# One ring of eight slots for the softmax weights of three attentions, with a planner that counts the slots

## The chip, the core and the metric

The kernel runs on one core of a Trainium2 chip. The metric is the device time of one execution in microseconds (us), as the median of several runs. Everything is computed in 32-bit floats.

## The reference

The input x is 8 images of 64 x 64 pixels with 256 channels. Two layers follow each other.

```
# layer 0
qkv = x @ w_qkv + b_qkv            # 256 -> 512, q and k; v is k
ctx_h = sdpa over 8 horizontal windows of 8 rows, channels 0..127, 4 heads of 32
ctx_v = sdpa over 8 vertical windows of 8 columns, channels 128..255, 4 heads of 32
hv  = hard_swish(v)
context = hard_swish(concat(ctx_h, ctx_v) + depthwise_conv3x3(hv) + dw_bias)
x = context @ w_out + b_out
# layer 1
f, g, h = x @ kf + bf, x @ kg + bg, x @ kh + bh     # 256 -> 32 each, spectrally normed
beta = softmax(g @ f.T)            # 4096 x 4096 per image
out = gamma * ((beta @ h) @ kv + bv) + x
```

Each window has 512 pixels, so a window of a head is a 512 x 512 attention. Layer 1 is a 4096 x 4096 attention with 32 channels.

## The kernel before

Scores are made transposed: keys stand on the 128 partitions, queries on the columns. A **step** is one block of 128 keys against 512 queries for four heads (layer 0) or four blocks of queries (layer 1), so 2048 columns of scores. In each step TensorE makes the scores in PSUM, ScalarE (ACT) turns them into weights with exponentials of 1024 columns each, TensorE multiplies the weights with the values into one accumulator `num`, and the sum of the weights is gathered for the division at the end. For an image there are

- 8 **h units** (horizontal windows, scores at L787, values at L816), 4 steps each, names `p_h`, `acc_h`, `num_h`, `sum_h`;
- 8 **v units** (vertical windows, scores at L764 and L787, values at L809 and L816). They have 3 steps: step 0 is as above with 2048 columns, steps 1 and 2 (`passes`) have 3072, written in three passes of 256 queries. Such a step uses three pairs of PSUM banks, `first`, `mid` and `last`, and gives two tiles of weights: `p_v` with 2048 columns (L776, L777) and the middle one `p_v_m` with 1024 (L781);
- 2 **l units** (layer 1, scores at L994, values at L1010), 32 steps each.

PSUM has six banks as three pairs for scores, one bank for the accumulator `num` and one, `mm`, for every other product. The scores of a step can only be written once the exponential has emptied their pair.

**Weights in SBUF before.** The pool `ptp` holds three buffers of 2048 columns (tag `pt`) for all steps in turn, and one of 1024 (tag `pm`) for the middle tile. A buffer may be written again when every reader of its last tile is done. Readers are: the value product (L809, L816, L1010); DVE's adds into `acc` (L825 `add` in h and v, L832 `add_mid` in v, L1025 in l), of which there is only one buffer as well; TensorE's sums with a matrix of ones (L847), which in v read step 2 and its middle tile directly; and in l the gather of the fourth row block by a DMA from POOL's queue that adds in flight into `acc_l` or `row_l` (L1036).

**Other work around it.** The projections of the next images (L298, tile `pq`), the depthwise convolution (nine taps, the first on ACT at L692, eight on DVE at L696), the hard swish, the normalizations (L558 to L561, L864), the joined context (L888 to L897), the projections to f, g and h (L917, L944) and the output (L298 into the score banks, then L1076) are put between the steps. f, g and h are staged in tiles with the tag `fgh` (two buffers of 512 columns; L926, L952) and copied on by DMA or transposed; output tiles have the tag `ot` (two buffers of 512 columns; L1076, L1103) and are stored by DMA.

**Order.** Image by image the units run h1 to h7, v0 to v7, then h0 of the next image, then l0 and l1. The program is written under a manual schedule, so each engine runs its instructions in the order in which the Python code issues them. A planner, the class `Flow`, sets that order: it keeps a modelled clock for each engine with fixed costs (in us: `SCORES`, `VALUES`, `EXP`, `ADD` and so on; `GATHER` and `SUMMED` for the gather by DMA), holds tasks with due times in lanes, and after each step fills the time until the PSUM banks come free. `step` issues scores and exponentials of a step, then the values of the step before, then the rest. For the middle tile, the exponential is issued by `rest` after those values.

Before it issues a step, the planner must have issued every reader of the tile that the new one takes the place of. It calls `flow.require` for the readers of step `t - 3`, and for the middle tile for those of the last middle tile. These readers are then in the order, but the modelled clock of ACT does not wait for their end: the exponential is modelled to end `EXP` after the scores or after ACT's last work.

Of the kernel before, what the change touches and what calls it, by code (L numbers as in the profile page):

```python
# [11 lines left out]
F32 = mybir.dt.float32  # L12
# [5 lines left out]
P = 128  # L18
# [3 lines left out]
TB = 512  # L22
NB = N // TB
D = 32
# [16 lines left out]
def side(h):  # L41
# [3 lines left out]
QH = 4  # L45

DUE = dict(
    near_k=-4, near_q=0, near_values=-14, clip=-12, swish=-1,
# [13 lines left out]
ADD, ADD3, NORM, SWISH, TAP, TAPS = 2.36, 1.83, 2.5, 0.75, 0.75, 1.28  # L62
GATHER, SUMMED = 1.0, 3.0
PE_LAG, LAG, SLACK = 0.28, 0.1, 0.3
# [3 lines left out]
class Task:  # L68
# [4 lines left out]
    def __init__(self, pieces, due=0, needs=(), after=(), ready=0, bank=False):  # L73
        self.pieces, self.due, self.ready = deque(pieces), due, ready
        self.needs, self.after, self.bank = list(needs), list(after), bank
        self.done, self.end = False, 0.0
        self.then = None
        self.ends = False

    def begin(self):  # L80
# [6 lines left out]
class Flow:  # L87
# [5 lines left out]
    def __init__(self):  # L93
        self.t = 0
        self.clock = dict(pe=0.0, act=0.0, dve=0.0, sp=0.0)
        self.lanes = dict(pe=[], turn=[], act=[], dve=[], sp=[], pool=[], rows=[], res=[])
        self.open = None
        self.held, self.held_more, self.values_due = None, 0.0, False
        self.bank_free = 0.0
        self.half_end = self.exp_end = 0.0  # L100
        self.third = False
        self.apart = 0
# [7 lines left out]
    def run(self, task):  # L110
        now = self.begin(task)
        fn, chain = task.pieces.popleft()
        fn()
        if task.then and len(task.pieces) <= task.then[0]:
            task.due = task.then[1]
        if task.lane == "sp":
            now = max(now, self.clock["pe"])
        for engine, took in chain:
            if engine in self.clock:
                now = max(now, self.clock[engine])  # L120
                self.clock[engine] = now + took
            now += took + (PE_LAG if engine == "pe" else LAG)
            if task.bank and engine in ("act", "dve"):
                self.bank_free = now
        task.end = now
        if task.bank:
            self.open = task if task.pieces else None
        if not task.pieces:
            task.done = True
            self.lanes[task.lane].remove(task)  # L130
# [5 lines left out]
    def require(self, *tasks):  # L136
        for task in tasks:
            task, left = task if isinstance(task, tuple) else (task, 0)
            while not task.done and len(task.pieces) > left:
                self.require(*task.needs, *task.after)  # L140
                if task.bank and self.open not in (None, task):
                    self.require(self.open)
                self.run(task)

    def waiting(self, lane):
# [79 lines left out]
    def step(self, scores, values, passes=2, third=False):  # L225
# [17 lines left out]
        if scores:  # L243
            rest = scores()
            c["pe"] = max(c["pe"], self.banks()) + DRAIN + SCORES + more
            self.third = third
            self.half_end = max(c["act"], c["pe"] - more + PE_LAG) + EXP
            if more:
                self.half_end = max(self.half_end, c["pe"] + PE_LAG) + EXP
            before, self.exp_end = self.exp_end, self.half_end + EXP  # L250
            c["act"] = self.exp_end
        else:
            before = self.exp_end
            c["pe"] = self.half_end = self.exp_end = max(c["pe"], c["act"], c["dve"]) + 3.0
# [11 lines left out]
        if rest:  # L266
            rest()
        self.fill_act(self.late(c["pe"]) - EVICT)
        self.fill_pe()
# [32 lines left out]
def tile_attention_blocks(  # L302
# [163 lines left out]
    def attention(images, load_x, out_rows, exact):  # L466
# [19 lines left out]
        f4 = state.tile([P, N], F32, name="f4")  # L486
        gq = state.tile([P, 2, TB], F32, name="gq")


# [54 lines left out]

        def weights_of(sc, name, scale):
            pt = ptp.tile([P, NQ, TB], F32, tag="pt", name=name)
            for z in range(2):
                nc.scalar.activation(pt[:, 2 * z : 2 * z + 2, :], sc[z], AF.Exp, scale=scale)  # L548
            return pt
# [40 lines left out]
        def image(b):  # L590
# [136 lines left out]
            def window_unit(kind, i):  # L727
# [26 lines left out]
                def scores(c):  # L754
                    q, k = sources(kind, i)
                    if exact and c == 0:
                        maxima()
                    name = f"p_{nm}_{c}"
                    if c in passes:
                        first, mid, last = sc = [pairs.popleft() for _ in range(3)]  # L760
                        pairs.extend((first, last, mid))
                        for n, (t, h) in enumerate(passes[c]):
                            for r in range(NQ):
# [9 lines left out]
                                if n == 2 and r == 0:  # L773
                                    handed(mm, relay)
                        pt = ptp.tile([P, NQ, TB], F32, tag="pt", name=name)
                        nc.scalar.activation(pt[:, :2, :], first, AF.Exp, scale=D**-0.5)  # L776
                        nc.scalar.activation(pt[:, 2:, :], last, AF.Exp, scale=D**-0.5)  # L777

                        def rest():
                            pm = ptp.tile([P, 2, TB], F32, tag="pm", name=f"{name}_m", bufs=1)  # L780
                            nc.scalar.activation(pm, mid, AF.Exp, scale=D**-0.5)  # L781
                            u[c], u["mid", c] = pt, pm
# [3 lines left out]
                    for r in range(NQ):  # L786
# [5 lines left out]
                        if exact:  # L792
# [4 lines left out]
                            )  # L797
                    u[c] = weights_of(sc, name, D**-0.5)
                    return None
# [107 lines left out]
            def fgh_tile(name):  # L907
                return work.tile([P, TB], F32, tag="fgh", name=f"{name}_{b}")

# [55 lines left out]
            def global_unit(z):  # L965
# [23 lines left out]
                def scores(c):  # L989
# [3 lines left out]
                    for r in range(NQ):  # L993
# [4 lines left out]
                        if exact:  # L998
# [4 lines left out]
                            )  # L1003
                    u[c] = weights_of(sc, f"p_{nm}_{c}", 1.0)

# [150 lines left out]

        readers = defaultdict(list)
        last_users = dict(acc=[], sum=[])
# [5 lines left out]
        def weights_ready(t):  # L1164
            task = Task([])
            task.done, task.step = True, t
            weights[t] = task
            return task

        weights = {}  # L1170
        for u in units:
# [32 lines left out]
            else:  # L1204
# [238 lines left out]

        mids = []
# [22 lines left out]
        with tc.manual_schedule():  # L1467
# [3 lines left out]
            for n, (u, c) in enumerate(steps):  # L1471
# [6 lines left out]
                if u.kind:  # L1478
                    weights[u.t + c].end = flow.exp_end + LAG
            if not exact:  # L1480
# [83 lines left out]
```

## Time and profile before

| | us |
|---|---|
| median of 3 runs | 3411.5 |
| lowest and highest | 3410.2, 3414.52 |
| the profiled execution | 3416.69 |
| its span on the core | 3414.9 |
| TensorE (PE) busy | 3309.1 (97%) |
| DVE busy | 2662.5 (78%) |
| ACT busy | 2669.1 (78%) |
| POOL busy | 518.4 (15%) |

The profile is of one execution, which was 5.2 us slower than the median of the runs shown; its span leaves out 1.8 us around it. Matmuls overlap and their ends are modelled, so a busy PE isn't PE at its peak: where that matters, the distance between starts is read. The granted TensorE clock had a mean of 0.994. "Idle before" a group of instructions is the time in which its engine stood still just before them, put down to what ended the wait.

### The profile page before, as it was taken

The numbers are of one execution on the slowest core, as the hardware profiler recorded it, in microseconds if no ns is written. First come the engines' busy times: TensorE is split into PE (matmuls) and PEld (weight loads), VectorE is DVE, ScalarE is ACT, GpSimd is POOL, SyncE is SP. The second block draws the span as 40 slices with busy tenths as digits, with TensorE's granted clock in tenths as the row PEclk, the third lists the DMA queues.
The fourth block names the chain that finished last, engine by engine and source line by source line (L and its number), as shares of the span: only waits on it lengthen the run. The fifth ranks groups of instructions, "written<-read, shape, count | busy, mean of one in ns | idle before, by whom it ended". The sixth has DMA issues, their size and how long they took to land. (4 is left out here: it accounts for less than half of the span.)

```text
span 3414.9 us, 82562 instructions
## 1 busy us (share of the span) xinstructions
PE 3309.1 (97%) x35348; PEld 1197.4 (35%) x35348; DVE 2662.5 (78%) x2404; ACT 2669.1 (78%) x3235; POOL 518.4 (15%) x776
## 2 busy tenths in 40 slices
PE   7889999999999999999999999999999999999998
PEld 3343333443334333343333433334333343333422
DVE  5778679876898758887598966988769886699865
ACT  5677787787877878778788787878877888778776
POOL 0001230012300123002230022200222003210032
PEclk9999999999999999999999999999999999999999
DMA  2123653245622555225552255423654236542365
GB/s 71 51 81 96 124 122 90 69 115 122 121 84 75 117 125 113 88 74 117 130 110 81 87 123 117 110 70 96 122 124 107 62 98 134 117 99 63 99 122 110
DMA packets 321111, 344.35 MB, mean 101 GB/s; under 512 B 34272, under 2 KB 198624, under 8 KB 320736
## 3 DMA queue, kind: packets, MB, share of 16 engines
q0 software_dynamic: 71680, 134.25, 22.3%
q1 hardware_dynamic: 246816, 204.18, 20.2%
q8 instruction: 280, 4.59, 0.6%
q10 hardware_dynamic: 2240, 0.56, 0.1%
q14 instruction: 95, 0.78, 0.1%
HBM read 99.78 MB, written 83.89 MB: 54 GB/s over the span
## 5 line engine op out<-in xcount | busy, mean ns | idle before, releaser
L548 ACT ACTIVATE p_l<-s 128x1024 f32<-128x1024 f32 x1024 | 994.0, 1027 | 175.4 <-PE s L994 137.6
L1025 DVE TENSOR_TENSOR acc_l<-acc_l,p_l 128x1536 f32<-128x1536 f32 x480 | 843.6, 1758 | 362.6 <-ACT p_l L548 357.8
L696 DVE SCALAR_TENSOR_TENSOR act<-hv,dw_sb,act 128x1024 f32<-128x1024 f32 x512 | 654.8, 1279 | 10.1
L994 PE MATMUL s<-gq,f 32*128 32x512 f32 x4096 | 616.2, 640 | 3.6 <-ACT p_l L548 3.4
L548 ACT ACTIVATE p_h<-s 128x1024 f32<-128x1024 f32 x512 | 495.6, 1023 | 104.3 <-PE s L787 70.4
L1010 PE MATMUL num_l<-p_l,h_sb 128*32 128x512 f32 x4096 | 546.3, 605 | 1.9 <-ACT nums_l L1040 1.9
L298 PE MATMUL pq<-x,wqkv_sb 128*32 128x256 f32 x8192 | 533.4, 381 | 12.8 <-ACT kv L641 8.4
L298 PEld LDWEIGHTS pq<-x,wqkv_sb 128*32 128x32 f32 x8192 | 264.3, 110 | 398.8 <-issue 250.2
L787 PE MATMUL s<-qh,kh 32*128 32x512 f32 x2048 | 307.1, 641 | 6.5 <-ACT qh L622 5.7
L1036 POOL DMA_DIRECT2D row_l<-p_l x240 | 219.1, 913 | 549.8 <-ACT p_l L548 493.0
L994 PEld LDWEIGHTS s<-gq,f 32*128 32x128 f32 x4096 | 179.7, 183 | 289.1 <-issue 270.6
L1036 POOL DMA_DIRECT2D acc_l<-p_l x240 | 211.0, 879 | 441.7 <-ACT p_l L548 406.3
L816 PE MATMUL num_h<-p_h,vs 128*32 128x512 f32 x2048 | 273.6, 606 | 3.8 <-DMA vs<-kvia 3.0
L764 PE MATMUL s<-qv,kv 32*128 32x256 f32 x3072 | 228.9, 399 | 4.1 <-ACT p_v L548 2.6
L298 PE MATMUL s<-act,wout_sb 128*32 128x512 f32 x2048 | 227.6, 594 | 0.2 <-ACT ot_l L1103 0.2
L1010 PEld LDWEIGHTS num_l<-p_l,h_sb 128*32 128x32 f32 x4096 | 80.7, 108 | 387.2 <-issue 372.6
L825 DVE TENSOR_TENSOR acc_h<-p_h,p_h 128x2048 f32<-128x2048 f32 x64 | 146.5, 2289 | 89.5 <-ACT p_h L548 51.7
L781 ACT ACTIVATE p_v_m<-s 128x1024 f32<-128x1024 f32 x128 | 131.6, 1028 | 98.8 <-DVE acc_v L832 59.5
L809 PE MATMUL num_v<-p_v,vs 128*32 128x256 f32 x2048 | 203.7, 390 | 0.0
L1076 ACT ACTIVATE ot_l<-s,bias_o 128x512 f32<-128x512 f32 x120 | 76.0, 685 | 151.0 <-PE s L298 143.1
L825 DVE TENSOR_TENSOR acc_v<-p_v,p_v 128x2048 f32<-128x2048 f32 x64 | 146.6, 2291 | 52.2 <-PE sum_v L847 45.0
L764 PEld LDWEIGHTS s<-qv,kv 32*128 32x128 f32 x3072 | 147.9, 185 | 95.2 <-issue 50.3
(146 smaller groups left out, 3551.8 us busy)
## 6 DMA issues: line engine op xcount, KB each, us to landing
acc_l<-p_l POOLq DMA_DIRECT2D x256, 256.0 KB, 3.4
row_l<-p_l POOLq DMA_DIRECT2D x256, 256.0 KB, 3.3
x<-in_xT SPq DMA_DIRECT2D x92, 512.0 KB, 4.1
kvia<-kt SPq DMA_DIRECT2D x128, 256.0 KB, 2.5
vs<-kvia SPq DMA_DIRECT2D x512, 64.0 KB, 2.1
out<-ot_l SPq DMA_DIRECT2D x128, 256.0 KB, 2.1
via_v<-nums_v SPq DMA_DIRECT2D x64, 256.0 KB, 2.1
shuf_v<-via_v SPq DMA_DIRECT2D x256, 64.0 KB, 2.1
```

The source lines that it names most:

```text
L298: nc.tensor.matmul(out[quad(r), :], lhsT=lhsT[:, quad(r)], rhs=rhs, start=start, stop=stop)
L548: nc.scalar.activation(pt[:, 2 * z : 2 * z + 2, :], sc[z], AF.Exp, scale=scale)
L696: nc.vector.scalar_tensor_tensor(o, src, wt, o, ALU.mult, ALU.add)
L764: mm = nc.tensor.matmul(place_of(n, r, h, sc), lhsT=k[quad(r), t * P : (t + 1) * P], rhs=q[quad(r), side(h)], start=True, stop=True,)
L787: nc.tensor.matmul(row_of(sc, r), lhsT=k[quad(r), c * P : (c + 1) * P], rhs=q[quad(r), :], start=True, stop=not exact,)
L809: nc.tensor.matmul(u["num"][quad(r), side(h)], lhsT=vs[kind, i][:, r, t, :], rhs=place_of(n, r, h, (pt[:, :2], u["mid", c], pt[:, 2:])), s ...
L816: nc.tensor.matmul(u["num"][quad(r), :], lhsT=vs[kind, i][:, r, c, :], rhs=u[c][:, r, :], start=(c == 0), stop=(c == 3),)
L825: nc.vector.tensor_add(u["acc"], u["acc"] if c == 2 else u[0], u[c])
L994: nc.tensor.matmul(row_of(sc, r), lhsT=f4[quad(r), c * P : (c + 1) * P], rhs=gq[quad(r), z, :], start=True, stop=not exact,)
L1010: nc.tensor.matmul(u["num"][quad(r), :], lhsT=h_sb[:, c, :], rhs=u[c][:, r, :], start=(c == 0), stop=(c == 4 * NB - 1),)
L1025: nc.vector.tensor_add(acc, u[0][:, :rows, :] if c == 1 else acc, u[c][:, :rows, :])
L1036: nc.gpsimd.dma_start(out=u["row", c % 2], in_=u[c][:, rows, :], accum_op=ALU.add)
```

## The change

All weights lie in one tile `weights` of eight slots of 1024 columns. A step takes two slots that follow each other; a step with passes takes three, and in a v unit these are laid out so that step 0 has slots 0 and 1, step 1 slots 2 and 3 with its middle in 4, step 2 slots 6 and 7 with its middle in 5. Eight slots of 4 KB take 32 KB of a partition. The three buffers of 8 KB and the one of 4 KB took 28; the 4 KB of the two `fgh` buffers are the rest, and f, g and h are now staged in the two `ot` buffers.

The planner walks the steps once ahead of time, gives each its slots, and notes for each slot which earlier step last had it and whether as a middle tile. Before a step it requires the readers of exactly those; `require` now also returns when they end by the modelled clock, and the end of the exponentials is modelled to be no earlier (`weights_free` for the first two, `mid_free` for the middle one). As a task can have several pieces, the end of each piece is noted in `times`. The costs `GATHER` and `SUMMED` of the model are set from 1.0 and 3.0 to 0.9 and 2.6.

```diff
+SLOTS = 8
-GATHER, SUMMED = 1.0, 3.0
+GATHER, SUMMED = 0.9, 2.6
...
-        task.end = now
+        task.end = task.times[len(task.pieces)] = now
...
     def require(self, *tasks):
...
+        ends = [k[0].times.get(k[1], k[0].end) if isinstance(k, tuple) else k.end for k in tasks]
+        return max(ends, default=0.0)
...
-            self.half_end = max(c["act"], c["pe"] - more + PE_LAG) + EXP
+            self.half_end = max(c["act"], c["pe"] - more + PE_LAG, self.weights_free) + EXP
...
         if rest:
             rest()
+            if self.mid_free > self.exp_end - EXP:
+                self.exp_end = c["act"] = self.mid_free + EXP
...
-        ptp = pools.enter_context(tc.tile_pool(name=f"ptp{sfx}", bufs=3))
...
+        weights = state.tile([P, SLOTS, 2, TB], F32, name="p")
...
+        def weights_at(slot, n=2):
+            return weights[:, slot : slot + n].rearrange("p s i c -> p (s i) c")
+
-            pt = ptp.tile([P, NQ, TB], F32, tag="pt", name=name)
+            pt = weights_at(next(slots)[0])
...
-                            pm = ptp.tile([P, 2, TB], F32, tag="pm", name=f"{name}_m", bufs=1)
+                            pm = weights_at(mid_at, 1)
...
-                return work.tile([P, TB], F32, tag="fgh", name=f"{name}_{b}")
+                return work.tile([P, TB], F32, tag="ot", name=f"{name}_{b}", bufs=out_bufs)
...
-                for c, task in enumerate((pair, pair, *held)):
+                first = (pair, 1) if u.passes else pair
+                for c, task in enumerate((first, first, *held)):
                     readers[u.t + c].append(task)
                 if u.passes:
-                    u.mids = {1: pair, 2: (total, 2) if acc is pair else acc}
+                    last_mids[u.t + 1] = pair
+                    last_mids[u.t + 2] = (total, 2) if acc is pair else acc
...
+        taken, order, old, place_at = {}, [], [], 0
+        for u in units:
+            for c in range(u.steps if u.kind else 0):
+                n = u.t + c
+                if u.kind in ("h", "v") and c in u.passes:
+                    at, mid_at = (place_at, place_at + 2) if c == 1 else (place_at + 1, place_at)
+                    place_at += 3
+                else:
+                    at, mid_at = place_at, None
+                    place_at += 2
+                assert place_at <= SLOTS
+                place_at %= SLOTS
+                order.append((at, mid_at))
+                before = [], []
+                for k, (slot, kept) in enumerate(((at, (n, 0)), (at + 1, (n, 0)), (mid_at, (n, 1)))):
+                    if slot is not None:
+                        if slot in taken:
+                            before[k // 2].append(taken[slot])
+                        taken[slot] = kept
+                old.append((n, before))
...
-                flow.require(*u.ahead.get(c, ()), *readers.pop(u.t + c - 3, ()))
+                flow.require(*u.ahead.get(c, ()))
+                flow.weights_free = flow.require(*left_by(old[u.t + c][0]))
...
-                flow.require(*mids)
-                mids[:] = [u.mids[c]]
+                flow.mid_free = flow.require(*left_by(old[u.t + c][1]))
                 rest()
```

More of the change, by code (lines that the diff above doesn't have):

```diff
@@ L78, in __init__ @@
         self.ends = False
+        self.times = {}
     def begin(self):
@@ L100, in __init__ @@
         self.half_end = self.exp_end = 0.0
+        self.weights_free = self.mid_free = 0.0
         self.third = False
@@ L487, in attention @@
         gq = state.tile([P, 2, TB], F32, name="gq")
+        weights = state.tile([P, SLOTS, 2, TB], F32, name="p")
+        slots = iter(())
         pairs = deque(ps_sc.tile([P, 2, TB], F32, name=f"s_{i}") for i in range(3))
@@ L543, in row_of, with weights_of @@
             return sc[r // 2][:, r % 2, :]
-        def weights_of(sc, name, scale):
-            pt = ptp.tile([P, NQ, TB], F32, tag="pt", name=name)
+        def weights_at(slot, n=2):
+            return weights[:, slot : slot + n].rearrange("p s i c -> p (s i) c")
+        def weights_of(sc, scale):
+            pt = weights_at(next(slots)[0])
             for z in range(2):
@@ L757, in scores @@
                         maxima()
-                    name = f"p_{nm}_{c}"
                     if c in passes:
@@ L774, in scores @@
                                     handed(mm, relay)
-                        pt = ptp.tile([P, NQ, TB], F32, tag="pt", name=name)
+                        at, mid_at = next(slots)
+                        pt = weights_at(at)
                         nc.scalar.activation(pt[:, :2, :], first, AF.Exp, scale=D**-0.5)
@@ L797, in scores @@
                             )
-                    u[c] = weights_of(sc, name, D**-0.5)
+                    u[c] = weights_of(sc, D**-0.5)
                     return None
@@ L1003, in scores @@
                             )
-                    u[c] = weights_of(sc, f"p_{nm}_{c}", 1.0)
+                    u[c] = weights_of(sc, 1.0)
                 def weighted(c):
@@ L1154, in attention @@
                 place(u, "l")
-        readers = defaultdict(list)
+        readers, last_mids = defaultdict(list), {}
         last_users = dict(acc=[], sum=[])
@@ L1166, in weights_ready @@
             task.done, task.step = True, t
-            weights[t] = task
+            made[t] = task
             return task
-        weights = {}
+        made = {}
         for u in units:
@@ L1442, in attention, with left_by @@
                     load(nxt, i, *near, nxt.far[i, 1], nxt.far[i, 3])
-        mids = []
+        taken, order, old, place_at = {}, [], [], 0
[18 more added lines that the diff above has]
+                old.append((n, before))
+        old = dict(old)
+        slots = iter(order)
+        def left_by(kept):
+            return [k for n, mid in kept for k in ([last_mids[n]] if mid else readers[n])]
         def unit_scores(u, c):
             if u.kind:
-                flow.require(*u.ahead.get(c, ()), *readers.pop(u.t + c - 3, ()))
+                flow.require(*u.ahead.get(c, ()))
+                flow.weights_free = flow.require(*left_by(old[u.t + c][0]))
                 if exact and c == 0 and flow.open:
@@ L1478, in attention @@
                 if u.kind:
-                    weights[u.t + c].end = flow.exp_end + LAG
+                    made[u.t + c].end = flow.exp_end + LAG
             if not exact:
```

## The prediction

> **What bounds the kernel now.** I began with the page's first part, the busy shares of the engines:
>
> ```profile
> PE 3309.1 (97%) x35348; PEld 1197.4 (35%) x35348; DVE 2662.5 (78%) x2404; ACT 2669.1 (78%) x3235; POOL 518.4 (15%) x776
> ```
>
> TensorE looks full, but this is a mean over stages that repeat eight times, and matmul ends are modelled. So I cut out one image, the fourth, at the first exponential of each stage, and asked for the busy time in three stretches: h (horizontal windows, 28 steps), v (vertical, 24 steps) and l (global attention, 64 steps).
>
> ```profile
> 1358.90:1466.80 107.90, 105.89 (x1068) 35.44 (x1060) 97.51 (x96) 83.12 (x101) 0.68 (x5) 1.00 0.25 77
> 1466.80:1563.30 96.50, 93.58 (x1232) 44.94 (x1232) 81.34 (x90) 76.62 (x92) 0.33 (x3) 0.98 0.30 86
> ...
> 1576.70:1775.40 198.70, 197.53 (x1992) 63.52 (x1992) 141.78 (x101) 161.89 (x198) 62.03 (x85) 1.00 0.61 124
> ```
>
> The columns are length, then PE, weight load, DVE, ACT and POOL busy. PE is near the whole length everywhere, so this alone separates nothing. What separates the stages is the distance from start to start on PE. In l it is tight:
>
> ```profile
> 1601.99 1.07 PE L1010 MATMUL num_l<-p_l,h_sb 128*32 128x512 f32 x8
> 1602.88 0.61 PE L298 MATMUL pq<-x,wqkv_sb 128*32 128x256 f32 x8
> 1603.42 1.14 PE L994 MATMUL s<-gq,f 32*128 32x512 f32 x8
> 1604.49 1.06 PE L1010 MATMUL num_l<-p_l,h_sb 128*32 128x512 f32 x8
> ```
>
> Values take 0.89 us, a projection piece 0.54, scores 1.07, and nothing lies between. Priced this way, l's 1992 matmul records are 1024 of scores and values (1.96 us per 16, 125 us), some 144 of the output product (an estimate from the page's counts, 2048 and 240 over eight images, half in l; 0.11 each, 16 us) and some 824 short ones (0.54 to 0.97 us per 8 to 16, so about 0.063 each, 52 us): 193 of 198.7 us. TensorE bounds l, with at most 6 us to win.
>
> In v it is not tight. One unit of the steady stretch, the starts on PE:
>
> ```profile
> 1510.01 1.58 PE L764 MATMUL s<-qv,kv 32*128 32x256 f32 x24
> ...
> 1512.95 1.36 PE L787 MATMUL s<-qv,kv 32*128 32x512 f32 x8
> 1514.24 0.63 PE L809 MATMUL num_v<-p_v,vs 128*32 128x256 f32 x4
> 1515.01 0.64 PE L809 MATMUL num_v<-p_v_m,vs 128*32 128x256 f32 x8
> ...
> 1516.42 2.15 PE L764 MATMUL s<-qv,kv 32*128 32x256 f32 x24
> 1518.51 1.07 PE L816 MATMUL num_v<-p_v,vs 128*32 128x512 f32 x8
> ...
> 1521.66 1.58 PE L764 MATMUL s<-qv,kv 32*128 32x256 f32 x24
> ```
>
> The period is 11.65 us. The same 24 score matmuls take 1.50 us at 1510.01 (values begin at 1511.51) and 2.09 at 1516.42. The 24 value matmuls take 1.44 us at 1511.51 and 2.18 at 1514.24, with a hole before 1515.01, where they need the middle weights p_v_m. So 0.59 + 0.74 + about 0.2 (the 512-column scores, 1.29 against 1.07) = 1.5 us of the period is waiting, and 10.1 is work. ScalarE at that place:
>
> ```profile
> 1513.93 1.02 ACT L781 ACTIVATE p_v_m<-s 128x1024 f32<-128x1024 f32 x1 [0.80 <-DVE acc_v L832]
> ```
>
> The exponential of the middle pair has its scores, but its buffer is the only one of its kind and DVE's add has not left it. ACT starts it 0.80 us late, the two exponentials behind it slip as well, and PE waits for all three. ACT's waits over the whole run (us in total, times, longest):
>
> ```profile
> ACT p_v_m L781 <- DVE acc_v L832: 59.5, 61, 3.0
> ACT p_v_m L781 <- PE sum_v L847: 37.9, 40, 1.3
> ...
> ACT p_h L548 <- DVE acc_h L825: 31.3, 26, 1.9
> ...
> ACT p_l L548 <- DMA acc_l<-p_l: 15.0, 9, 2.0
> ...
> ACT p_l L548 <- DVE acc_l L1025: 8.9, 11, 1.2
> ...
> ACT p_l L548 <- DMA row_l<-p_l: 4.7, 7, 1.6
> ```
>
> These six are the waits for a weight buffer, 157 us; every other large wait of ACT is for PE's results and has nothing to do with the change.
>
> **The change part by part.**
>
> *Ring instead of three big buffers and one small.* Eight slots of 1024 columns: a v unit uses 2 + 3 + 3 = 8, an h unit 4 x 2 = 8, an l step 2. A middle slot is reused three steps later where it was one or two, an h or l slot four steps later where it was three. No activation, matmul or add is added or removed.
>
> v, the wait behind acc_v (59.5 us): the middle slot of step 2 was last read a unit (about 11 us) ago, so the wait goes. Following the unit above by hand: the middle exponential starts at 1513.13 and not 1513.93, its values no longer hold PE (0.74 back), and the next exponentials come 0.8 earlier, which gives most of the 0.59 back, because PE then waits for the last bank only. What is late next is ACT's last exponential and DVE. I take 0.75 to 0.8 of a us per unit, 64 units: 48 to 51 us.
>
> v, the wait behind sum_v (37.9 us): it goes too, but at 1519.39 to 1521.66 PE is busy with the sums without a gap, and the exponential released is needed only after them. The cover is those sums; I take 0. If the cover were gone it could bring 38.
>
> h (31.3 us): ACT stands there 26 times, DVE being the late one, busy 97.5 of 107.9 us. Half reaches PE, as PE is nearly full: 12 us taken, between 0 and 31.
>
> l (15.0 + 8.9 + 4.7 = 28.6 us): PE is never short in the rows above. Taken: 4 us, between 0 and 28.6. Here a rule weighs against my reading. The Trainium skill, page "Perfetto Trace Analysis", section "Identifying the Most-Contended Engine", says not to judge TensorE's headroom by matmul busy time but by the weight-load share. That share is 63.5/198.7 = 32% in l and 44.9/96.5 = 47% in v, so by the rule l has more room than v and its 28.6 us could come back in full. The start-to-start row says at most 6 us per image for everything. I follow the row; by the rule the sum would be some 25 us larger.
>
> *Waits on ACT's queue.* With one tile, every exponential and not only the first of a tile has its own list of earlier readers and writers. In the built programs ACT has 2204 semaphore instructions after and 1245 before, and 759 exponentials (138 before) have TensorE's signal in such an instruction ahead of them and a wait for an older activation, eight or more back and long done, in themselves. Nothing new is waited for. What an instruction of this kind costs:
>
> ```profile
> L548 ACTq EVENT_SEMAPHORE  x688: 17/38/2767, 36.6 to 3381.2; - x172
> ```
>
> 17 or 38 ns where nothing is outstanding, and it runs under the activation before it. Where ACT really waits for PE, the trace shows an activation 22 ns after PE's signal if it waits itself, and 45 ns after the end of the semaphore instruction if that one waits: some 0.04 us more. Exponentials released by PE are 478 in ACT's waits (263 + 127 + 88); with 759/2048 of all in the slow form, 177 x 0.045 = 8 us. Ends: 0 (all hidden) and 759 x 0.045 = 34 us. I take +8.
>
> *f/g/h staging in the result buffers.* Two result buffers of the same size serve both. Results (L1076) are written in the second half of l and the first half of h; in the image above they stop before 1410 and begin again after 1674, and f/g/h (L926, L952) lie between 1527 and 1599. The gap of over 70 us on either side hides the handover; 51 more semaphore instructions are in the count above. 0 us; if the two met, one store's landing (2.1 us) per tile.
>
> *Planner.* GATHER and SUMMED fall to 0.9 and 2.6: the trace has 0.87 us per gather and 3.3 to landing. In the built program the order on PE within v is as before. Per image, 16 matmul instructions (one projection, 4 x 0.43 = 1.7 us) move from h to l; on DVE five taps leave h, four go to v and one to l, and one normalization (0.71 + 0.25 + 0.71 + 0.69 = 2.36 us) moves from v to h. DVE in h: 97.5 - 6.4 - 0.7 (a swish) + 2.4 = 93; in v: 81.3 + 5.1 - 2.4 = 84. On PE the move is even, h loses what l gains. In v DVE also puts the normalization of the unit before ahead of the add, which makes it wait for ACT's copy of the sums, about 0.7 us per unit: 84 + 6 = 90 us per v stage. That is the next bound: 96.5 - 6 = 90.5, what the wait removed gives. SP's and POOL's queues keep their DMAs, 1506 and 512.
>
> Sum: -49 (v) - 12 (h) - 4 (l) + 8 (semaphores) = -57. The profiled execution took 3416.7 us (span 3414.9), 5.2 above the median 3411.5; 3416.7 - 57 - 5.2 = 3354.5, so 3355 us.
>
> **The rivals.**
>
> *DVE takes over in v.* For it: 84 us of work plus waits in a stage that shall last 90. If half of v's and h's gain is lost so: -25 - 6 + 8 = -23, 3389 us. Against it: acc_v is needed only at the next unit's sums, some 3 us later even in the new order.
>
> *More than the sum.* If h's and l's waits reach the end in full and v gets its 1.5 us per unit: v 96 and h and l 8 more than forecast, with semaphores hidden: about -105, 3307 us. Against it: no stage of h or l shows such holes on PE.
>
> *Slower: the semaphore instructions.* Place: ACT ahead of each exponential that waits for PE, in l and h above all, where PE waits for the bank that ACT empties. Price: up to 34 us; the projection moved into l, which is full, adds 1.7 x 7 = 12. It decides once v returns less than 46 us, that is under 0.7 us per unit with h and l giving nothing; with 0.45 per unit (29 us) the run is 17 us longer, 3428. Against it: those instructions mostly run ahead, under an activation of 1.02 us.
>
> *No change:* the new wait is for DVE at the same places. Only if both effects cancel, 3411.
>
> **How the numbers follow.** Forecast 0.66 (3330 to 3382), DVE in v 0.13, more 0.09, slower 0.08, no change 0.04. Differences under 0.2% (7 us) can't be told from none. The range 3315 to 3398 holds the forecast and the DVE case and part of the larger gain; left out are slower, no change and the far end. Faster is 0.66 + 0.13 + 0.09 = 0.88, same 0.04, slower 0.08.
>
> **What would show it.** Right: ACT's waits for acc_v and sum_v at the middle exponential are nearly gone, v lasts 90 to 91 us, a steady unit about 10.8, l within 2 us of 198.7, h 104 to 107. DVE in v above 90% of the stage. Wrong: v unchanged with ACT or PE waiting for DVE there; or l longer by 4 us or more per image with activations late behind semaphore instructions; or h shorter by far more than 4 us.

## Result and profile after: faster, by a third of the forecast

The changed kernel takes 3392.97 us (median of 5 runs, 3392.09 to 3395.03) and the one before 3411.5 (5 runs): ratio 0.9947, 95% interval 0.9933 to 0.9962. That is 18.5 us less where 57 were forecast. The profiled span is 3390.2 us.

The busy shares of the page of the changed kernel say nothing about the place:

```profile
PE 3295.3 (97%) x35348; PEld 1196.2 (35%) x35348; DVE 2658.9 (78%) x2404; ACT 2662.6 (79%) x3235; POOL 557.5 (16%) x776
```

The fourth image again, in four stages: h, v, the four steps of the next image's h unit (called h0), and l. The stretches that the prediction shows lie 11 us too late. In the kernel before, the first exponential of v is this one, and not one at 1466.8:

```profile
1455.78 1.94 ACT L548 ACTIVATE p_v<-s 128x1024 f32<-128x1024 f32 x2
```

All borders are off by the same 11 us, so the lengths hold, but the busy times are those of other stretches. Cut at the first exponentials, the kernel before has

```profile
1347.90:1455.80 107.90, 106.04 (x1044) 33.76 (x1042) 93.87 (x90) 83.59 (x104) 4.31 (x11) 1.00 0.28 83
1455.80:1552.30 96.50, 92.89 (x1220) 45.21 (x1216) 86.25 (x94) 75.74 (x92) 0.33 (x3) 0.98 0.30 85
1552.30:1565.70 13.40, 13.35 (x148) 5.12 (x148) 8.22 (x10) 11.11 (x15) 0.00 (x0) 1.00 0.26 73
1565.70:1764.40 198.70, 198.13 (x2008) 63.88 (x2006) 143.06 (x106) 162.60 (x199) 60.46 (x82) 1.00 0.61 126
```

and the changed one (the columns are length, PE, weight load, DVE, ACT, POOL)

```profile
1340.20:1442.50 102.30, 102.07 (x1012) 32.40 (x1010) 88.08 (x86) 80.53 (x100) 4.91 (x7) 1.00 0.28 83
1442.50:1535.80 93.30, 91.03 (x1192) 44.90 (x1192) 88.01 (x93) 76.09 (x93) 0.33 (x3) 1.00 0.29 86
1535.80:1552.70 16.90, 15.76 (x184) 5.94 (x180) 8.18 (x9) 11.91 (x16) 0.00 (x0) 1.00 0.20 51
1552.70:1753.50 200.80, 200.39 (x2038) 64.96 (x2030) 146.78 (x113) 163.51 (x200) 66.36 (x86) 1.00 0.62 128
```

v looks 3.2 us shorter, but it has 28 matmul records fewer (1192 against 1220), and h0 has 36 more and is 3.5 us longer: that is work that crossed the border. The two must be read together, 109.9 before and 110.2 after. They gained nothing. h is 5.6 us shorter, 1.7 of it the projection that went to l, and l 2.1 us longer.

The six waits for weight buffers of before have become these (ACT's waits: us in total, times, longest):

```profile
ACT sum_sb_v L580 <- PE sum_v L859: 45.8, 40, 2.1
ACT p L560 <- DVE acc_v L837: 35.5, 29, 3.4
...
ACT p L560 <- DVE acc_l L1037: 21.2, 13, 2.5
ACT p L560 <- DVE acc_h L837: 19.3, 16, 3.1
```

The waits at the middle exponential (97 us before) are gone but for 0.4 us, as forecast. In their place the exponentials of step 0 (L560) wait for the add into acc_v, 35.5 us, and the copy of the sums waits 45.8 us (9.4 before).

The fourth v unit, v3, shows how. First TensorE, from its step-0 values to the next unit's:

```profile
1480.45 1.06 PE L828 MATMUL num_v<-p,vs 128*32 128x512 f32 x8
...
1489.32 0.70 PE L775 MATMUL s<-qv,kv 32*128 32x256 f32 x4
1490.28 0.71 PE L775 MATMUL s<-qv,kv 32*128 32x256 f32 x8 [0.26 <-ACT p L560]
1491.20 1.13 PE L775 MATMUL s<-qv,kv 32*128 32x256 f32 x12 [0.20 <-ACT p L560]
1492.26 1.07 PE L828 MATMUL num_v<-p,vs 128*32 128x512 f32 x8
```

The period is 11.81 us; the same unit took 11.69 before. The 24 score matmuls come in three bits, each after an exponential, and take 2.94 us where 1.5 is enough. Then ACT in the same stretch:

```profile
1483.79 0.59 ACT L580 COPY sum_sb_v<-sum_v 128x512 f32<-128x512 f32 x1 [1.22 <-PE sum_v L859]
...
1489.20 1.94 ACT L560 ACTIVATE p<-s 128x1024 f32<-128x1024 f32 x2 [0.90 <-DVE acc_v L837]
```

and DVE, whose order explains both:

```profile
1484.41 0.71 DVE L570 STREAM_TRANSPOSE zt_v<-sum_sb_v 128x512 f32<-128x512 f32 x1 [0.24 <-ACT sum_sb_v L580]
1485.16 0.26 DVE L572 RECIPROCAL recs<-zt_v 128x16 f32<-128x16 f32 x1
1485.45 0.71 DVE L573 STREAM_TRANSPOSE sum_sb_v<-recs 128x512 f32<-128x512 f32 x1
1486.19 0.69 DVE L876 TENSOR_TENSOR nums_v<-nums_v,sum_sb_v 128x512 f32<-128x512 f32 x1
1486.80 2.29 DVE L837 TENSOR_TENSOR acc_v<-p 128x2048 f32<-128x2048 f32 x1
```

The normalization of the unit before now stands ahead of the add that reads step 0's and step 1's weights; the exponential of the next step 0 needs the slots that this add leaves. So there is a closed loop: sums on PE end (1483.7), copy on ACT (to 1484.4), normalization (to 1486.8), add (to 1489.1), two exponentials (to 1491.1), last scores (to 1492.3), values and sums (to 1495.5). From one end of the sums to the next, 11.8 us. No engine needs to be full for it. DVE is nearly full in this unit all the same (the third busy time, 11.36 of 11.81 us):

```profile
1480.45:1492.26 11.81, 11.35 (x146) 5.49 (x144) 11.36 (x13) 9.23 (x12) 0.00 (x0) 1.00 0.31 94
```

So a full DVE looks as likely a cause as the loop; the light taps below decide between the two. Three of the eight v units, v1 to v3, have this period.

### The profile page after: what moved, and what is told of

It is laid out like the page before. It is cut to its first block, busy times and chain, and to the rows that moved or that the text cites. A ratio compares the mean times of both kernels' runs of the same rounds, so it can differ in the third digit from the quotient of the medians.

```text
span 3390.2 us, 83413 instructions
## 1 busy us (share of the span) xinstructions
PE 3295.3 (97%) x35348; PEld 1196.2 (35%) x35348; DVE 2658.9 (78%) x2404; ACT 2662.6 (79%) x3235; POOL 557.5 (16%) x776
## 4 chain that ended last, share of the span: by engine, by line
PE 80%; DVE 9%; ACT 5%; issue 3%; DMA 1%; SPq 0%; ACTq 0%; DVEq 0%
PE s L1006 15%; PE num_l L1022 13%; PE pq L306 12%; PE s L799 9%; PE s L306 7%; PE num_h L828 6%; PE s L775 4%; PE sum_v L859 4%; PE sum_h L859 3%; DVE act L708 3%; ACT p L560 3%; PE num_v L821 3%; DVE acc_v L837 2%; PE num_v L828 2%; PE pf L929 1%
## 5 line engine op out<-in xcount | busy, mean ns | idle before, releaser
L560 ACT ACTIVATE p<-s 128x1024 f32<-128x1024 f32 x1664 | 1611.7, 1025 | 295.5 <-PE s L1006 144.5
L1037 DVE TENSOR_TENSOR acc_l<-acc_l,p 128x1536 f32<-128x1536 f32 x480 | 842.9, 1756 | 346.9 <-ACT p L560 342.8
L1022 PE MATMUL num_l<-p,h_sb 128*32 128x512 f32 x4096 | 546.5, 605 | 1.9 <-ACT nums_l L1052 1.9
L1048 POOL DMA_DIRECT2D row_l<-p x240 | 211.1, 879 | 505.1 <-ACT p L560 483.9
L1048 POOL DMA_DIRECT2D acc_l<-p x240 | 212.6, 886 | 447.7 <-ACT p L560 388.8
L828 PE MATMUL num_h<-p,vs 128*32 128x512 f32 x2048 | 273.3, 605 | 4.6 <-DMA vs<-kvia 2.7
L775 PE MATMUL s<-qv,kv 32*128 32x256 f32 x3072 | 251.4, 402 | 18.5 <-ACT p L560 16.8
L837 DVE TENSOR_TENSOR acc_h<-p 128x2048 f32<-128x2048 f32 x64 | 146.2, 2284 | 111.6 <-ACT p L560 62.3
L821 PE MATMUL num_v<-p,vs 128*32 128x256 f32 x3072 | 192.3, 383 | 0.0
L837 DVE TENSOR_TENSOR acc_v<-p 128x2048 f32<-128x2048 f32 x64 | 146.4, 2287 | 28.1 <-ACT act L704 15.4
L837 DVE TENSOR_TENSOR acc_h<-acc_h,p 128x2048 f32<-128x2048 f32 x64 | 146.0, 2282 | 13.1 <-ACT p L560 13.1
```

The costliest lines, as they stand in the source:

```text
L775: mm = nc.tensor.matmul(place_of(n, r, h, sc), lhsT=k[quad(r), t * P : (t + 1) * P], rhs=q[quad(r), side(h)], start=True, stop=True,)
L821: nc.tensor.matmul(u["num"][quad(r), side(h)], lhsT=vs[kind, i][:, r, t, :], rhs=place_of(n, r, h, (pt[:, :2], u["mid", c], pt[:, 2:])), s ...
L828: nc.tensor.matmul(u["num"][quad(r), :], lhsT=vs[kind, i][:, r, c, :], rhs=u[c][:, r, :], start=(c == 0), stop=(c == 3),)
L837: nc.vector.tensor_add(u["acc"], u["acc"] if c == 2 else u[0], u[c])
L1022: nc.tensor.matmul(u["num"][quad(r), :], lhsT=h_sb[:, c, :], rhs=u[c][:, r, :], start=(c == 0), stop=(c == 4 * NB - 1),)
L1037: nc.vector.tensor_add(acc, u[0][:, :rows, :] if c == 1 else acc, u[c][:, :rows, :])
```

## The experiments

All times per image below are means over the second to seventh image, read from each kernel's trace between the first exponentials of the stages.

| kernel | us | h | v + h0 | l | image | first image |
|---|---|---|---|---|---|---|
| before | 3411.5 | 108.0 | 109.7 | 199.0 | 416.7 | 514.5 |
| after | 3393.0 | 102.3 | 110.2 | 200.8 | 413.4 | 513.5 |
| ring, old order | 3351.2 | 105.9 | 105.1 | 198.1 | 409.1 | 500.3 |
| old buffers, new planner | 3435.9 | 103.3 | 112.6 | 204.8 | 420.7 | 513.3 |
| two middle buffers, old order | 3360.6 | 108.0 | 103.1 | 199.1 | 410.2 | 506.3 |
| after, acc_v first | 3356.5 | 102.4 | 105.4 | 200.9 | 408.7 | 510.3 |
| after, mid requirement back | 3354.4 | 102.4 | 102.9 | 201.5 | 406.8 | 518.4 |
| after, no slot clock | 3374.0 | 104.9 | 105.4 | 198.9 | 409.2 | 521.7 |
| after, norm later | 3367.6 | 102.3 | 104.3 | 200.9 | 407.5 | 517.1 |
| after, all adds first | 3351.9 | 103.0 | 105.6 | 200.8 | 409.3 | 504.3 |
| both repairs | 3340.5 | 102.9 | 102.8 | 201.6 | 407.2 | 501.0 |

"First image" is everything from the start of the span to the second image's h stage. Ratios and intervals are given with each experiment.

**The ring with the old order.** The slots and their requirements stay; the planner's costs, its requirements of before and its clock are put back.

```diff
-GATHER, SUMMED = 0.9, 2.6
+GATHER, SUMMED = 1.0, 3.0
...
-                flow.require(*u.ahead.get(c, ()))
-                flow.weights_free = flow.require(*left_by(old[u.t + c][0]))
+                flow.require(*u.ahead.get(c, ()), *readers.get(u.t + c - 3, ()))
+                flow.require(*left_by(old[u.t + c][0]))
...
-                flow.mid_free = flow.require(*left_by(old[u.t + c][1]))
+                flow.require(*mids)
+                mids[:] = [u.mids[c]]
+                flow.require(*left_by(old[u.t + c][1]))
```

> The ring of eight slots and the shared staging, with the old planner (its costs, its requirements, no clock for slots): apart from 12 matmuls in the first image, every engine has the order of before. Theory A (the ring takes the wait away, and the new order on DVE, which puts taps and a normalization ahead of acc_v, brings it back at the next unit's step 0): v and the four steps of h behind it, 109.9 us before and 110.2 after in the fourth image, fall to 103 to 106; the whole is 3355 to 3375 us. Theory B (DVE is full in v, so that no order helps): v and h0 stay at 109 to 110, the whole 3395 to 3410 us.

3351.17 us, ratio 0.9818 (0.9805 to 0.9832): the ring by itself gives 62 us, a little more than the whole forecast, and 4 us better than theory A's range. In the trace ACT, DVE and POOL run in exactly the order of before. DVE's work is the same, so a full DVE isn't the reason.

**The planner without the ring.** The four old buffers; `weights_free` and `mid_free` from the same readers as before, and the new costs.

> The four old buffers, with the planner's clock now held until they come free and the new costs GATHER and SUMMED: the planner's part without the ring. Theory A: h gains as in the change (some 3 to 5 us per image less), v and h0 not; 3380 to 3400 us. Theory B: the same as before within 0.3%, 3400 to 3415 us, if the gain in h came from the ring.

3435.88 us, ratio 1.0064 (1.005 to 1.0078), slower, which neither expectation had. h is 4.7 us shorter as in the change, v and h0 2.9 longer and l 5.8 longer. The h gain of the change thus looks like mostly the new order's. The order here is not quite that of the change, because other readers are required, so this is likely and not shown. What makes v, h0 and l longer here was not traced.

**The old costs.** GATHER and SUMMED alone put back.

> The changed kernel with GATHER and SUMMED at 1.0 and 3.0 as before. Both theories: these two costs decide little, 3385 to 3400 us; a difference over 7 us would say that the result hangs on how the planner happens to fall and not on the slots.

3392.82 us, ratio 0.994 (0.9927 to 0.9954): the costs do nothing. The trace has the order of the change on PE, ACT, DVE and POOL.

**acc_v first.** In the changed kernel the adds into acc_v are due eight steps earlier, so DVE takes them ahead of the normalization and the taps.

```diff
-acc = pair = flow.add("dve", pieces, u.t + 2, w[:2], ready=u.t + 2)
+acc = pair = flow.add("dve", pieces, u.t + 2 - (8 if u.kind == "v" else 0), w[:2], ready=u.t + 2)
```

> The changed kernel, with the due time of the two adds into acc_v eight steps earlier, so that DVE takes them as soon as the weights and acc are there, ahead of taps and the normalization of the unit before. Theory A: the 0.9 us wait of the exponentials of step 0 for acc_v (35.5 us in all) goes, v and h0 take 103 to 106 us in place of 110.2, the whole 3340 to 3365 us. Theory B: DVE is as full as before, what it puts first makes something else late; v and h0 109 to 111 us, the whole 3385 to 3400 us.

3356.53 us, ratio 0.9833 (0.982 to 0.9847), v and h0 105.4: as theory A had it. One due time returns 36 of the missing 38 us. h0 stays as long as in the change (17.0 us), and v alone falls from 93.3 to 88.4.

**The requirement for the middle tile back.** Before step 2's middle exponential, step 1's adds must have been issued, as with one middle buffer.

```diff
+flow.require(*([last_mids[u.t + 1]] if c == 2 else []))
 flow.mid_free = flow.require(*left_by(old[u.t + c][1]))
```

> The changed kernel, and ahead of the middle exponential of step 2 of a v unit the planner again requires that both adds of step 1 into acc_v have been issued, as it did when there was one middle buffer. Nothing else differs. Theory A (the requirement that the ring makes unnecessary was what kept acc_v early in DVE's order): v and h0 fall from 110.2 us to 104 to 107 per image, the whole is 3350 to 3370 us. Rival (the planner's clock for slots, not the dropped requirement, made the bad order): v and h0 stay at 109 to 111, the whole 3385 to 3400 us.

3354.40 us, ratio 0.9829 (0.9816 to 0.9843), v and h0 102.9, 1 us below the expected range. The requirement that the ring made unnecessary had kept the add early on DVE. With it PE, too, has its order of before again in v and h0.

**No clock for the slots.**

> The changed kernel without the clock for slots: readers are required as in the change, but the model takes the exponentials to start without waiting for them (weights_free and mid_free stay zero). Theory A: the dropped requirement does the harm, so this one keeps it; v and h0 109 to 112 us, the whole 3385 to 3410 us. Rival (the clock made the order): 3350 to 3370 us.

3374.03 us, ratio 0.988 (0.9865 to 0.9895): neither range. v and h0 fall to 105.4, so the dropped requirement alone does not make the bad order in the later images; it takes the clock as well. The first image is 8 us longer than in the change. How the two act together was not traced further.

**Two middle buffers, nothing else.** The kernel before with `bufs=2` for the middle tile, and f, g and h in the result buffers; order on every engine as before.

> The kernel before with two middle buffers in place of one, and f, g and h staged in the result buffers, which makes room for it: the same SBUF as the change, the order on every engine as before, the three big buffers kept. It separates v from the rest of the ring's gain. If the middle buffer was the whole of v: v 92 us as with the ring in the old order (96.3 before), h and l as before (108.0, 199.0); 3365 to 3385 us. If the gain of the ring in v needed separate slots for the rest as well: 3395 to 3410 us.

3360.59 us, ratio 0.9846 (0.9832 to 0.9859). v falls from 96.3 to 89.8, h and l stay. So 53 of the ring's 62 us are one 4 KB buffer; the first expectation held, and the time is 4 us better than its range. Per image the whole ring is only 1.1 us better than this: h and l gain 2.1 and 1.0, but v and h0 take 2.0 longer, mostly because the second v unit's first exponentials then wait for DVE's add (2.4 us in the fourth image, 0.8 here).

**Light taps.** The order of the changed kernel; each tap on DVE leaves out seven eighths of its rows.

```diff
-nc.vector.scalar_tensor_tensor(o, src, wt, o, ALU.mult, ALU.add)
+nc.vector.scalar_tensor_tensor(o[:, :2], src[:, :2], wt, o[:, :2], ALU.mult, ALU.add)
```

> The changed kernel, order on every engine the same, but each of the eight convolution taps on DVE does 2 of its 16 rows (the rest of the tap is left out), some 0.2 us in place of 1.28. It tells whether it is time of DVE ahead of acc_v that holds v, or the order on TensorE and ScalarE. Theory A (DVE work in front of acc_v): the 0.9 us waits of step 0 for acc_v are gone, v and h0 fall from 110.2 to 101 to 104 us per image. Rival (the new order on PE, with the sums and the projections to f and g where they now are, costs the gain): v and h0 stay above 107 us.

v and h0 stayed at 110.2: my expectation failed, and the cause that I had written into theory A with it. PE (first two lines) and DVE (last two) of this kernel's timeline:

```profile
1445.68 1.07 PE L828 MATMUL num_v<-p,vs 128*32 128x512 f32 x8
...
1457.48 1.07 PE L828 MATMUL num_v<-p,vs 128*32 128x512 f32 x8
```

```profile
1449.64 0.71 DVE L570 STREAM_TRANSPOSE zt_v<-sum_sb_v 128x512 f32<-128x512 f32 x1 [3.85 <-ACT sum_sb_v L580]
...
1452.03 2.29 DVE L837 TENSOR_TENSOR acc_v<-p 128x2048 f32<-128x2048 f32 x1
```

DVE is idle for 3.85 us in such a unit, waits for the copy of the sums, and the period is 11.80 us as before. The taps are not in the way in these units: they lie in the loop's slack. (One run, 3371.2 us; the time saved is in the first and last image and l.)

**Light normalization.** Same order again; the two last operations of v's normalization leave out all but 64 of 512 columns (`n` is 2 in v), and the copy of `num` on ACT scales by a constant.

```diff
-                rt.unsqueeze(2).to_broadcast([P, TB // D, D]),
+                rt[:, :n].unsqueeze(2).to_broadcast([P, n, D]),
...
-                    nc.vector.tensor_mul(num, num, u["sum"])
+                    nc.vector.tensor_mul(num[:, : n * D], num[:, : n * D], u["sum"][:, : n * D])
```

> The changed kernel, order on every engine the same, but in v units the second transpose and the product of the normalization do 64 of their 512 columns (the rest of the division is left out, the copy of num scales by 1/800 in its place), about 1.1 us less per unit on DVE. Theory C (closed loop through the normalization): the steady unit of 11.8 us falls by about 1.1 to 10.7, in the units that have that order; v and h0 106 to 108 us. If the loop isn't what holds v: 110 us, as with the light taps, which took away more DVE time than this.

```profile
1460.25 1.07 PE L828 MATMUL num_v<-p,vs 128*32 128x512 f32 x8
...
1471.12 1.07 PE L828 MATMUL num_v<-p,vs 128*32 128x512 f32 x8
```

```profile
1465.24 0.24 DVE L573 STREAM_TRANSPOSE sum_sb_v<-recs 128x64 f32<-128x64 f32 x1
1465.52 0.23 DVE L880 TENSOR_TENSOR nums_v<-nums_v,sum_sb_v 128x64 f32<-128x64 f32 x1
1465.66 2.28 DVE L837 TENSOR_TENSOR acc_v<-p 128x2048 f32<-128x2048 f32 x1
```

The period on PE is 10.87 us, 0.94 less, and v and h0 of the fourth image take 107.4. The two operations took 0.71 and 0.69 us in the change, so 0.93 us of DVE came out of the loop (1.1 was expected), and the period fell by as much; 2.8 us of taps (three of them, 3.92 us in the change and 1.12 with light taps) taken out beside it did nothing. With the same order on PE and DVE in all three kernels, that shows the loop. (One run, 3374.7 us.)

**Normalization later.** It is due two steps later in v, so that the add passes it; the taps keep their place.

> The changed kernel with the normalization of a v unit due two steps later, so that the planner lets DVE take the add into acc_v before it; taps and all else keep their due times. Theory C, after the light taps changed nothing in v: a closed loop holds v, from the end of the sums on PE over their copy on ACT, the normalization and the add on DVE, to the exponentials of step 0, the last scores and the sums again (11.8 us), and the normalization is the part that need not be in it. Then v and h0 fall from 110.2 to 103 to 106 us, the whole 3345 to 3365 us. If it was the taps in front of the add after all: v and h0 108 or more, over 3380 us.

v and h0 104.3, as theory C has it; 3367.61 us in all, ratio 0.9866 (0.9849 to 0.9882), 3 us over the range; the first image is 4 us longer than in the change and the last 6.

**All adds first, and both repairs together.** The adds of h (`pair` and the third step's) also due eight steps earlier; then that with the requirement back.

> The changed kernel with the adds into acc due eight steps earlier in h as well as in v. Theory A: the waits of the exponentials for acc_h (19 us) go like those for acc_v; 2 to 3 us less than the 3356.5 us with acc_v alone, unless DVE in h (90% busy) then makes the normalizations late: 3345 to 3365 us. If h has no room: 3360 to 3375 us.

> The requirement for the middle slot back and the adds into acc_h and acc_v due eight steps earlier, both on the changed kernel: the two repairs together. If they mend the same thing, as theory A has it: 3342 to 3356 us, per image the 407 us of the first repair, with the first image shorter as with the second. If they mend different things the gains add: below 3340 us.

3351.93 us, ratio 0.982 (0.9807 to 0.9834), and 3340.46 us, ratio 0.9786 (0.9773 to 0.9799), the best of all. The first lies in its range for another reason than expected: h did not gain (103.0 us, against 102.4 with acc_v alone), the first image did (6 us). The second lies just between its two ranges; per image it is as with the first repair and in the first image as with the second. ACT's waits in the last one, then its fourth image's v and h0, then DVE in a steady unit:

```profile
ACT p L560 <- DVE acc_h L837: 7.4, 7, 1.1
ACT p L560 <- DVE acc_v L837: 1.6, 2, 0.9
```

```profile
1418.10:1507.70 89.60, 88.93 (x1221) 44.92 (x1218) 83.61 (x91) 76.61 (x92) 0.33 (x3) 1.00 0.32 92
1507.70:1520.90 13.20, 13.20 (x148) 4.97 (x148) 12.99 (x12) 10.51 (x13) 0.00 (x0) 1.00 0.26 75
```

```profile
1455.69 2.29 DVE L837 TENSOR_TENSOR acc_v<-p 128x2048 f32<-128x2048 f32 x1 [0.47 <-PE sum_v L859]
1458.09 1.23 DVE L844 TENSOR_TENSOR acc_v<-acc_v,p 128x1024 f32<-128x1024 f32 x1
1459.23 0.70 DVE L570 STREAM_TRANSPOSE zt_v<-sum_sb_v 128x512 f32<-128x512 f32 x1
```

Here the add starts right after the sums and the normalization follows it. Over v and h0 together DVE is busy for 94% of the time (87% in the change), and they are 7.4 us shorter: DVE's share of a stage was no sign of what holds it.

**Where the 7.4 us lie.** The v units of the fourth image one by one, in us from first exponential to first exponential:

| kernel | v0 | v1 | v2 | v3 | v4 | v5 | v6 | v7 and h0 |
|---|---|---|---|---|---|---|---|---|
| before | 12.9 | 12.4 | 11.1 | 11.7 | 11.7 | 12.2 | 11.1 | 26.9 |
| after | 11.3 | 11.8 | 11.8 | 11.8 | 10.8 | 12.2 | 11.1 | 29.4 |
| after, acc_v first | 9.9 | 10.4 | 10.8 | 10.8 | 10.8 | 12.1 | 11.2 | 29.5 |
| after, norm later | 11.3 | 10.3 | 10.8 | 10.8 | 10.8 | 12.1 | 10.8 | 27.4 |
| after, light norm | 11.3 | 10.9 | 10.9 | 10.9 | 10.8 | 12.2 | 11.1 | 29.4 |
| both repairs | 9.9 | 10.4 | 10.8 | 10.8 | 10.8 | 12.1 | 11.2 | 26.8 |

The loop is in v1 to v3 and costs 3.4 us per image. In v0 the add into acc_v stands behind the normalization of the last h unit, and the next exponential waits 1.45 us for it; acc_v first takes that away too. The other 2.6 us, in v7 and h0, are not DVE's order. From the sums of v6 on, the change has another order on PE than the kernel before. The five kernels here that have PE's order of before throughout v and h0 take 26.8 to 27.0 us on average for this part (before, ring in the old order, two middle buffers, mid requirement back, both repairs), and the six that have the order of the change 29.4 to 29.5 (after, old costs, acc_v first, all adds first, light taps, light norm). A part of it can be seen in the trace of the change:

```profile
1539.86 0.66 PE L970 MATMUL ph<-ident,h 128*128 128x128 f32 x4
1540.45 1.06 PE L828 MATMUL num_h<-p,vs 128*32 128x512 f32 x8
1542.49 1.50 PE L859 MATMUL sum_v<-p,ones 128*32 128x512 f32 x16 [0.98 <-ACT h_sb L971]
```

The product `ph` and the sums share one PSUM bank, so the sums wait until ACT has copied `ph` out. Here only eight value products stand between the two; with both repairs there are 24 of v, eight scores and eight of h, and PE does not wait. The rest of the 2.6 us was not traced.

## Why the prediction was right in direction and wrong in size

- **The middle buffer's wait (-49 us).** Right, place and size: two middle buffers alone give 53 us. The unit of 10.8 us that was forecast (v4, 11.65 before) is there too, in the change itself and in both repairs.
- **The rest of the ring in h and l (-16) and the semaphores (+8).** The ring in the old order is 9 us faster than the two middle buffers; the net forecast was 8. That is in part luck: h's part was 2.1 us per image and l's 1.0, and v and h0 gave 2.0 of it back, which was not forecast.
- **Semaphores by themselves.** Take the exponentials that had stood idle for over 0.25 us and that PE released. In the trace of the change they start 22 ns (median) after PE's signal where they wait themselves, and 82 ns after it where a semaphore instruction ahead does the waiting. The second form occurs 54 times, and 48 times before, where I had reckoned with 177 more. The extra is 0.06 us and not 0.045, but of too few: under 1 us where I took 8. The slower rival's price isn't in the trace.
- **The planner (0 us), the step that failed.** I took PE's order within v to be that of before, which it is only up to the sums of v6, and the order on DVE as a sum of busy time: "in v DVE also puts the normalization of the unit before ahead of the add", priced at 0.7 us of waiting per unit. The move was seen and its price was wrong, because I asked who waits for DVE's total and not who waits for that add. I even wrote that acc_v is needed only at the next unit's sums. The accumulator is; the slots that the add reads are needed by the next step 0's exponentials, some 5 us earlier (1489.2 against 1494.4 in the unit shown), and by them the sums that the normalization waits for. Measured, in place of 0: the change minus the ring in the old order, +42 us, of which one requirement returns 39. Against both repairs the change loses 4.8 us per image by DVE's order in v0 to v3, and 2.6 in v7 and h0, where the kernels with the change's order on PE are the slow ones.
- **The busy times of the stages.** The stretches began 11 us late, so the sums for DVE were wrong: it has 93.9 us in h and 86.3 in v, and not 97.5 and 81.3. With these, the same working gives DVE 86.3 + 5.1 - 2.4 + 6 = 95 us in v, more than the 90.5 that were to remain. So even as a sum of busy time DVE's order could not be put at nothing. The readings from start to start on PE and of single waits aren't touched; l has 2008 matmul records and not 1992, which adds 1 us to its 193.
- **"DVE takes over in v".** Its number (3389 us) is near the result, its mechanism is refuted: with the taps cut to an eighth v is the same, and with DVE busier over v and h0 (94% against 87%) they are faster. That the number is near is luck. For the same reason "DVE in v above 90% of the stage" was no sign of being right: the change has 88.0 of 93.3 us.
- **The rule and the row.** l's waits (29 us) came back at 0.9 us per image with the ring in the old order, about 7 us over the run and not 29: the distance between starts was the better guide than the weight-load share. (The Trainium skill, "Perfetto Trace Analysis", section "Identifying the Most-Contended Engine", names the share of the peak flop rate, MFU, beside that share; the prediction left it out, and no run here weighs it.)
- **h and l.** h fell by 5.7 per image (3 forecast with the moved projection), l rose by 1.8 (1.2 forecast). Of h, the ring in the old order gives 2.1, where 1.5 were forecast for it, and the old buffers with the new planner gain 4.7 without any ring.

Left open: the first image. Its length ranges from 500 to 522 us over these orders, and 13 of the 42 us that the order costs lie there. In the change ACT waits there once 7.1 us for a tap before it may clip into a reused buffer, and not in the two kernels with all adds first, which are 9 to 13 us shorter there. But the kernel with the old buffers and the new planner has no such wait either and is as long there as the change, so this wait isn't shown to be the cause.

## What to carry to other kernels

When a buffer is added, the wait that it removes may have been doing a second job: here its requirement made the planner issue the reader early. Before counting the gain, follow the reader's new place in its engine's order, list all that waits for it, and close the loop: if the chain comes back to its start, its length is the period, however idle the engines are. To tell a full engine from a loop, make an operation beside the chain light and then one in it: here only the second changed the period.

## What the runs showed that was not expected

v and h0 with DVE busy 87% of the time ran slower than with 94%. Cutting every convolution tap on DVE from 1.28 to 0.35 us left v and h0 at 110.2 us, while 0.93 us per unit out of the normalization shortened the loop by 0.94. One requirement of the planner had been dropped because no buffer needed it; put back, it mends the order on two engines, DVE's in v0 to v3 and PE's in v7 and h0. And a semaphore instruction ahead of an activation that waits for PE costs 0.06 us on its start.
